# Four graph-attention layers on one core: a planner that knows transfer-behind-transfer and GpSimd-behind-VectorE waits, and a last feed-forward in column pieces

## The chip, the cores and the metric

The kernel runs on one core of a Trainium2 chip. The metric is the time of one execution on the device in microseconds; several executions give a median.

## The reference

The input x has 16 batches of 1024 nodes with 256 features, and adj is one 1024x1024 graph. Each of four layers adds a graph network of the normalized input to x:

```python
h = jnp.maximum(_layernorm(x, axis=-1), 0.0)
x = x + layer(h, adj, ...)
```

Layers 0 to 2 are graph attention (layer 0 with 4 heads of 64, layers 1 and 2 with one head of 256): project h, form scores from a source and a destination term with a leaky slope, mask with adj, softmax over the neighbours, weighted sum of the projected rows, then elu (layers 0, 2) or relu (layer 1). Layer 3 is a transformer block with 8 heads of 32:

```python
scores = jnp.where(mask, jnp.einsum('fnhd,fmhd->fhnm', q, k) / jnp.sqrt(D), -1e9)
t = jnp.einsum('fhnm,fmhd->fnhd', softmax(scores), v).reshape(F, N, C)
x = _layernorm(x + t, ln1_g, ln1_b)
h = jax.nn.relu(x @ w1 + b1)
x = _layernorm(x + h @ w2 + b2, ln2_g, ln2_b)
```

## The kernel before, in words

All work is recorded first and issued later. Each piece of work is a `Work` with an engine, an estimated time, the buffers it writes and reads, and a stream with a position. `Record.add` finds what each piece must follow. `Record.schedule` then plays the program through: it repeatedly takes the engine that can start something earliest, and on it the piece with the lowest key (the batch number plus a curve from `KNOTS` over the position in its stream, less a `LEAD`). What it plays is the order in which each engine's instructions are issued. [...] . `PASS` holds what the planner allows for handing a result from one engine to another. `SLACK` is added to each transfer, and `SWITCH` and `BIAS` price a change of the tile shape on TensorE.

Queues: SP issues all loads and stores. GpSimd issues the accumulating transfers of L1287 and runs small additions and the power -0.5 (L468, L483), which turns variances into inverse deviations.

Batches overlap: while one batch is in attention (layer 3) and its feed-forward, later batches are in layers 0 to 2. The names used below:

- Layers 0 to 2: `hn` is the normalized input, turned by TensorE (L531) and copied by ScalarE to `hT` (L788); L794 projects it; L805 and L816 evict into `e` and `qb`; L893 forms masked weights `pt` from a row `row` broadcast by SP (L876); L1007 and L1017 (layer 0, 128x32 tiles) and L920 (layers 1 and 2, full tiles) multiply; L940 to L977 finish and add to `xh`.
- Attention: L1157 projects keys and queries, L1166 and L1169 split them into `hi` and `lo`, SP stores them to `hl` (L1175) and loads them back in another arrangement as `qs` and `ks` (L1181). L1386 forms scores in four banks `sc`, L1410 takes exponentials into `pa`, L1419 masks them, L1243 multiplies with values and ones in 128x32 tiles, L1270, L1278 and L1287 add up pairs for the denominators. L1326, L531, L1346, L1353 and L1366 turn back, divide and add.
- Feed-forward (`feed`): L480, L483 and L492 give the inverse deviation, L502 normalizes, L531 turns, L1470 makes `yT`; L1483 multiplies with w1, L1504 evicts with relu into `fz`, L1483 multiplies with w2, L1521 adds to `yT` on VectorE. Then `back` turns `yT` (L531), evicts with sums (L1567, L448), and L1586 and L1599 combine with `xr`.
- `xr` is the residual of two node tiles: SP loads it from `x3` in HBM (L1536), VectorE adds the bias row (L1542), L1599 adds the result, SP stores it to the output (L1608). There are two `xr` buffers, so the load of a pair must wait for the store of the pair before the last.

The rule that decides which dependencies cost a hand-over in the plan is, for a writer behind earlier readers:

```python
for y in readers:
    if y is not x:
        x.before.setdefault(y, y.engine != engine)
```

In the plan all SP transfers belong to one engine, "dma".

Of the kernel before, what the change touches and what calls it, by code (L numbers as in the profile page):

```python
# [115 lines left out]
WEIGHT = {"pe": 1.0, "dve": 0.3}  # L116
PASS = {"pe": 0.198, "act": 0.161, "dve": 0.218, "pool": 0.13, "dma": 0.0}

# [25 lines left out]
class Record:  # L144
# [12 lines left out]
    def add(self, engine, us, emit, w=(), r=(), modes=("full", "full"), key=None, moved=0.0, lands=0.0):  # L157
# [4 lines left out]
        for wrote, refs in ((False, r), (True, w)):  # L162
            for ref in refs:
# [7 lines left out]
                for q in list(buf.parts) if part is None else {part, None}:  # L171
                    if q not in buf.parts:
                        continue
                    writer, readers = buf.parts[q]
                    if writer is not None and writer is not x:
                        x.before[writer] = x.before.get(writer, False) or (writer.engine, engine) != ("pe", "pe")
                    if wrote:
                        for y in readers:
                            if y is not x:
                                x.before.setdefault(y, y.engine != engine)  # L180
                if wrote:
# [7 lines left out]
    def schedule(self):  # L189
# [49 lines left out]

        order = []  # L240
        while True:
# [14 lines left out]
            if e == "pe":  # L256
                us += SWITCH.get((mode, x.modes[0]), 0.0)
                mode = x.modes[1]
            x.start = at
            if x.moved:  # L260
# [21 lines left out]
BEHIND, HELD = 2.0, 1.35  # L282
SLACK = 0.944
KNOTS = {
    "gat0": (-8.057, -7.567, -4.564, -6.528, -1.817, -1.899, -1.452, -3.246, -8.552),
    "gat1": (-2.024, -0.004, 0.215, 0.731, 0.959, 0.704, 0.611, 0.917, 0.899),
    "gat2": (1.118, -0.917, 0.633, 0.85, 0.97, 0.804, 1.307, 1.739, 1.201),
    "beside": (-0.565, 3.144, 4.806, -3.201, 8.62),
    "values": (-3.421, -4.341, -3.452, -4.286, -2.082, -2.123, 4.475, -0.299, 0.523),
    "steps": (-0.249, 0.878, 1.095, 1.509, 1.61, 1.967, 1.973, 2.318, 0.345),  # L290
    "feed": (4.232, 4.502, 1.869, 1.3, 2.54, 0.571, -2.425, 2.126, 2.697),
    "last": (4.663, 0.548, 4.755, 0.436, 4.627, 5.109, 4.463, 6.627, 6.529),
}
BIAS = 4.008
LEAD = {"act": 4.014, "dve": -5.116}

# [13 lines left out]
def tt_us(n):  # L310
    return (n / 0.96 + 67) / 1000


def stt_us(n):
    return (n / 0.96 + 128) / 1000

# [12 lines left out]
def direct(ctx, tc, flag, x, adj, gat_w, gat_a, w_qkv, ln1_g, ln1_b, ln2_g, ln2_b, w1, b1, w2, b2, out):  # L329
# [125 lines left out]
    def inverse_of_squares(mean, squares, rstd, refs, rstd_ref, negate=True):  # L455
# [10 lines left out]
        pool(  # L466
            1.6,
            lambda: nc.gpsimd.tensor_tensor(  # L468
# [8 lines left out]
    def inverse(mean, var, rstd, mv_refs, rstd_ref, negate=True):  # L477
# [3 lines left out]
        pool(  # L481
            1.6,
            lambda: nc.gpsimd.tensor_tensor(  # L483
# [23 lines left out]
    def watch(b_rec, view, k):  # L507
# [3 lines left out]
        pool(  # L511
            0.524,
            lambda: nc.gpsimd.tensor_tensor(
# [235 lines left out]
    def gat(xt, b_mv, b_rstd, l, my, squared):  # L749
# [8 lines left out]
        for hf in range(2):  # L758
# [76 lines left out]
            if H == 1:  # L835
# [6 lines left out]
            pool(  # L842
                1.0,
                lambda: nc.gpsimd.tensor_tensor(
# [63 lines left out]
        for hf in range(2):  # L908
# [83 lines left out]
            for h in range(0, H, 2):  # L992
# [64 lines left out]
                def sums():  # L1057
# [10 lines left out]
                dve(  # L1068
                    tt_us(HALF),
                    lambda: nc.vector.tensor_mul(  # L1070
# [36 lines left out]
    def attention(b, xt, b_mv, b_rstd):  # L1107
# [42 lines left out]
        def project(g, hf, keys, stack, at):  # L1150
# [4 lines left out]
            def product():  # L1155
# [11 lines left out]
            dve(  # L1167
                tt_us(HALF),
                lambda: nc.vector.tensor_sub(lo.t, sc.t, hi.t),  # L1169
# [88 lines left out]
        for n in range(len(steps) + LAG):  # L1258
# [62 lines left out]
            if m >= 0 and steps[m][2] == NT - 1:  # L1321
# [17 lines left out]
                def turned(u):  # L1339
# [11 lines left out]
                dve(  # L1351
                    tt_us(HALF),
                    lambda: nc.vector.tensor_mul(  # L1353
# [78 lines left out]
    def feed(b, x3, hn):  # L1432
# [4 lines left out]
        def turn(hf):  # L1437
# [18 lines left out]
            for ct in range(CT):  # L1456
# [22 lines left out]
                )  # L1479

        def product(g, co, w_sb, src):
            for ct in range(CT):
                nc.tensor.matmul(  # L1483
                    g.t,
                    w_sb[:, ct, co * P : (co + 1) * P],
                    src(ct),
                    start=ct == 0,
                    stop=ct == CT - 1,
                )

        def forward(hf):
            yT = yTs[hf]
            fT = [r_fz.new() for _ in range(CT)]
            for co in range(CT):
                g = r_bank.new()
                pe(
                    CT * mm_us(HALF),
                    lambda: product(g, co, w1_sb, lambda ct: yT.t[:, ct, :]),
                    [g, fT[co]],
                    [yT],  # L1500
                )
                act(
                    act_us(HALF, 1),
                    lambda: nc.scalar.activation(  # L1504
                        fT[co].t, g.t, AF.Relu, bias=cols["b1"][:, co : co + 1]
                    ),
                    [fT[co]],
                    [g],
                )
            for co in range(CT):  # L1510
                g = r_bank.new()
                pe(
                    CT * mm_us(HALF),
                    lambda: product(g, co, w2_sb, lambda ct: fT[ct].t),
                    [g],
                    fT,
                )
                u = yT.t[:, co, :]
                dve(
                    stt_us(HALF),  # L1520
                    lambda: nc.vector.scalar_tensor_tensor(  # L1521
                        u, g.t, cols["b2"][:, co : co + 1], u, op0=ALU.add, op1=ALU.add
                    ),
                    [yT(co)],
                    [g],
                )

        def back(hf):
            yT = yTs[hf]
            for it in (hf * TH, hf * TH + 2):  # L1530
# [31 lines left out]

                pe(0.109 * 2 * CT, turn_back, [g], [yT])
                for k in range(2):
# [744 lines left out]
```

## Time and profile before

| | us |
|---|---|
| median of three runs | 4072.89 (4071.52 to 4074.02) |
| profiled execution, its own time | 4064.23 |
| its span | 4062.4 |
| TensorE busy | 3971.5 |
| VectorE busy | 3617.2 |
| ScalarE busy | 2666.1 |
| GpSimd busy | 718.9 |

The profile is of one execution, 8.66 us below the median. Matmuls are pipelined and their ends are modelled, so a matmul that is held up counts as busy. Rows of the timeline give start, duration, engine, line, operation, operands, and in brackets the idle time of that engine just before, with what ended it. "SPq" is the issue of a transfer by SP.

### The profile page before, as it was taken

To read this page: it belongs to the slowest core of one execution; us is meant where nothing else is said; L and a number is where in the kernel's file an instruction comes from. 1 tells how busy PE (TensorE), PEld (TensorE's weight loads), DVE (VectorE), ACT (ScalarE), POOL (GpSimd) and SP (SyncE) were. 2 spreads that over 40 slices of the span, in tenths; PEclk is the share of its full clock that TensorE was granted. 3 is DMA by queue.
4 is the path that set the end of the run, shared out by engine and by line. 5 is a ranking of instruction groups with operands and counts; after the bars stand their busy time and mean duration, and the time that the engine had idled before them with its cause. 6 is when DMAs were issued, how large, how long until landed. Compare 5 with 4: busy or idle time off the path is not lost. (4 is left out here: it accounts for less than half of the span.)

```text
span 4062.4 us, 64901 instructions
## 1 busy us (share of the span) xinstructions
PE 3971.5 (98%) x23394; PEld 2330.7 (57%) x23394; DVE 3617.2 (89%) x6130; ACT 2666.1 (66%) x6639; POOL 718.9 (18%) x631
## 2 busy tenths in 40 slices
PE   7999999999999999999999999999999999999998
PEld 3556466564665646556565665646656465564653
DVE  7769998999989899898999999899998998989976
ACT  5356576675766757567665776757667575675675
POOL 1001121211212212121111212112122121211110
PEclk9999999999999999999999999999999999999999
DMA  3054454444544445354454544445444453544542
GB/s 128 24 148 115 120 135 110 103 106 117 136 112 104 107 120 133 104 124 107 111 121 121 133 115 100 106 117 133 115 104 104 118 137 104 122 103 103 124 130 60
DMA packets 228666, 460.65 MB, mean 113 GB/s; under 512 B 24816, under 2 KB 59888, under 8 KB 228336
## 3 DMA queue, kind: packets, MB, share of 16 engines
q1 hardware_dynamic: 193776, 330.58, 29.0%
q0 software_dynamic: 34560, 125.84, 16.0%
q8 instruction: 186, 3.05, 0.3%
q14 instruction: 144, 1.18, 0.1%
HBM read 229.45 MB, written 101.06 MB: 81 GB/s over the span
## 5 line engine op out<-in xcount | busy, mean ns | idle before, releaser
L1419 DVE TENSOR_TENSOR pa<-pa,mask 128x1024 f32<-128x1024 f32 x1024 | 1228.0, 1217 | 85.1 <-ACT pa L1410 83.4
L1410 ACT ACTIVATE pa<-sc 128x512 f32<-128x512 f32 x2048 | 1102.1, 602 | 296.7 <-PE sc L1386 206.5
L893 DVE SCALAR_TENSOR_TENSOR pt<-row,e,mask 128x512 f32<-128x512 f32 x1472 | 1008.0, 745 | 54.4 <-DMA row<-rd 38.9
L920 PE MATMUL bank<-qb,pt 128*128 128x257 f32 x4096 | 947.7, 381 | 1.6 <-DVE pt L893 1.4
L920 PEld LDWEIGHTS bank<-qb,pt 128*128 128x128 f32 x4096 | 772.5, 190 | 164.0 <-issue 23.3
L1386 PE MATMUL sc<-qs,ks 128*128 128x512 f32 x2048 | 742.3, 463 | 7.3 <-ACT pa L1410 5.5
L1243 PE MATMUL bank<-pa,va 128*32 128x512 f32 x4096 | 517.1, 598 | 0.1
L1386 PEld LDWEIGHTS sc<-qs,ks 128*128 128x128 f32 x2048 | 363.9, 189 | 196.3 <-ACT pa L1410 77.2
L1007 PE MATMUL bank<-pt,qb 128*32 128x512 f32 x3840 | 468.5, 598 | 2.7 <-DVE pt L893 1.5
L794 PE MATMUL bank<-w_aug,hT 128*128 128x259 f32 (+1 forms) x1504 | 388.6, 395 | 15.3 <-ACT hT L788 7.4
L1287 POOL DMA_DIRECT2D sums<-pa x240 | 213.9, 893 | 902.7 <-DVE pa L1419 269.5
L794 PEld LDWEIGHTS bank<-w_aug,hT 128*128 128x128 f32 x1504 | 273.6, 190 | 161.5 <-ACT pa L1410 26.0
L948 ACT ACTIVATE ex<-bank,rec 128x256 f32<-128x256 f32 x256 | 118.5, 474 | 344.0 <-DVE rec L940 343.8
L1270 DVE TENSOR_TENSOR sums<-pa,pa 128x1024 f32<-128x1024 f32 x240 | 289.1, 1220 | 26.5 <-PE bank L1243 26.5
L1278 DVE TENSOR_TENSOR sums<-sums,pa 128x1024 f32<-128x1024 f32 x240 | 290.9, 1218 | 21.1 <-DMA sums<-pa 21.0
L468 POOL TENSOR_TENSOR rstd<-rstd,neg_half 128x4 f32<-128x4 f32 x94 | 159.2, 1694 | 747.6 <-DVE rstd L460 747.6
L1007 PEld LDWEIGHTS bank<-pt,qb 128*32 128x32 f32 x3840 | 118.6, 110 | 283.9 <-issue 225.0
L1017 PE MATMUL bank<-pt,e 128*32 128x512 f32 x1920 | 257.6, 594 | 0.0
L1243 PEld LDWEIGHTS bank<-pa,va 128*32 128x32 f32 x4096 | 113.9, 109 | 249.1 <-issue 224.8
L1157 PE MATMUL sc<-hTa,wqkv_sb 128*128 128x512 f32 x512 | 243.4, 598 | 0.0
L1038 ACT COPY ot<-bank 128x512 f32<-128x512 f32 x120 | 70.3, 587 | 200.0 <-PE bank L1007 168.3
L502 ACT ACTIVATE hn<-xh,mv,rstd 128x256 f32<-128x256 f32 x376 | 197.8, 604 | 5.7 <-DVE mv L492 4.1
(153 smaller groups left out, 4695.3 us busy)
## 6 DMA issues: line engine op xcount, KB each, us to landing
sums<-pa POOLq DMA_DIRECT2D x240, 512.0 KB, 5.6
ks<-hl SPq DMA_DIRECT2D x256, 256.0 KB
qs<-hl SPq DMA_DIRECT2D x256, 256.0 KB
row<-rd SPq DMA_DIRECT2D x184, 256.0 KB
hl<-hi SPq DMA_DIRECT2D x128, 256.0 KB
hl<-lo SPq DMA_DIRECT2D x128, 256.0 KB
xh<-in_x_dram SPq DMA_DIRECT2D x32, 512.0 KB
x<-xh SPq DMA_DIRECT2D x32, 512.0 KB
```

Source lines behind the costliest of these rows:

```text
L794: nc.tensor.matmul(g.t[:, : C + 3 * H], hT.t[:, ct, k * P : (k + 1) * P], w_aug[l][:, ct, :], start=ct == 0, stop=ct == CT - 1,)
L893: lambda: nc.vector.scalar_tensor_tensor(pt.t, row.t, e3[:, 2, jt // TH, h, jt % TH : jt % TH + 1], mask[:, jt, hf * HALF : (hf + 1) * HAL ...
L920: nc.tensor.matmul(g.t[:, : D + 1], pts[jt].t[:, k * P : (k + 1) * P], qb[:, jt, 0, :], start=jt == 0, stop=jt == NT - 1,)
L1007: nc.tensor.matmul(g.t[u * D + d : u * D + d + D3, :], qb[:, j, h + u, d : d + D3], pts[u][j - jt].t, start=j == 0, stop=j == NT - 1,)
L1017: nc.tensor.matmul(gd.t[c : c + D3, :], one(jt + k, h + u).to_broadcast([P, D3]), pts[u][k].t, start=jt == 0, stop=jt == NT - 2,)
L1157: nc.tensor.matmul(sc.t, wqkv_sb[:, ct, c0 : c0 + P], hT.t[:, ct, hf * HALF : (hf + 1) * HALF], start=ct == 0, stop=ct == CT - 1,)
L1243: nc.tensor.matmul(ac.t[r * D3 : (r + 1) * D3, :], columns(r), of_head(r), start=first, stop=last,)
L1270: lambda: nc.vector.tensor_add(ss.t, p0.t, p1.t),
L1278: lambda: nc.vector.tensor_add(ss.t, ss.t, pt.t),
L1386: nc.tensor.matmul(scs[r - r0].t, ks.t[:, r, jt * P : (jt + 1) * P].bitcast(F32R), q.t[:, r, :].bitcast(F32R), start=True, stop=True,)
L1410: lambda: nc.scalar.activation(pt.t[:, v, :], sc.t, AF.Exp, scale=1.0 / math.sqrt(D3)),
L1419: lambda: nc.vector.tensor_mul(pt.t, pt.t, mask[:, jt : jt + 1, i0 : i0 + HALF].to_broadcast([P, 2, HALF]),),
```

## The change

It has three parts.

1. The planner. A writer that follows a transfer which reads its buffer is now planned to wait for that transfer's completion, even where the writer is itself a transfer. VectorE work with two operands in SBUF, and GpSimd additions and powers, carry a time of type `Port`. Where a GpSimd `Port` piece starts while a VectorE `Port` piece runs, the plan holds GpSimd until that VectorE instruction ends, or longer if another one follows at once. VectorE work that reads PSUM is marked `float`.
2. The constants: `PASS`, `SLACK`, `KNOTS`, `BIAS`, `LEAD` and the times of GpSimd's operations have other values. So the order on every engine is another one. Outside the last batch the same instructions are issued, transfers included.
3. In the last batch (b = 15) the products of the feed-forward are computed for 256 columns at a time: two pieces for each half of the nodes. Products, evictions (L1504) and additions (L1521) are made once for each piece, and the transposes behind them need only the piece that holds their columns.

```diff
-PASS = {"pe": 0.198, "act": 0.161, "dve": 0.218, "pool": 0.13, "dma": 0.0}
+PASS = {"pe": 0.156, "act": 0.266, "dve": 0.175, "pool": 0.13, "dma": 0.0}
+
+class Port(float):
+    pass
...
-                                x.before.setdefault(y, y.engine != engine)
+                                x.before.setdefault(y, y.engine != engine or y.moved > 0)
...
+        def hold(us):
+            free["pool"] += us
+            for y in held.after:
+                t = free["pool"] + held.pass_on
+                if held in y.before and y.before[held] and t > y.ready:
...
+                    y.ready = t
...
+            if e == "pool":
+                held = None
+                if isinstance(us, Port) and locked and free["dve"] > at:
+                    held, since, edge, long = x, at, free["dve"], last > 1.0
+                    us += edge - at - 0.05
+            if e == "dve":
+                locked = isinstance(us, Port)
+                if held:
+                    if locked and at <= edge + 0.02 and (edge - since < 0.35 or long and us > 1.0):
+                        hold(us)
+                        edge, long = at + us, us > 1.0
+                    else:
+                        held = None
+                last = us
...
-SLACK = 0.944
+SLACK = 0.748
...
-BIAS = 4.008
-LEAD = {"act": 4.014, "dve": -5.116}
+BIAS = 3.411
+LEAD = {"act": 1.749, "dve": -1.422}
...
 def tt_us(n):
-    return (n / 0.96 + 67) / 1000
+    return Port((n / 0.96 + 67) / 1000)
...
         pool(
-            1.6,
+            Port(0.4 + 0.15 * n),
...
+        PARTS = 2 if b == NB - 1 else 1
+        W = HALF // PARTS
...
+            for q in range(PARTS):
+                w = slice(q * W, (q + 1) * W)
+                for co in range(CT):
+                    g = r_bank.new()
+                    pe(
+                        CT * mm_us(W),
+                        lambda: product(g, co, w1_sb, lambda ct: yT.t[:, ct, w]),
+                        [g, fT[co](q)],
+                        [yT],
+                    )
...
+            for q in range(PARTS):
+                w = slice(q * W, (q + 1) * W)
+                for co in range(CT):
+                    g = r_bank.new()
+                    pe(
+                        CT * mm_us(W),
+                        lambda: product(g, co, w2_sb, lambda ct: fT[ct].t[:, w]),
+                        [g],
+                        [f(q) for f in fT],
+                    )
...
-                pe(0.109 * 2 * CT, turn_back, [g], [yT])
+                q = it % TH // 2 if PARTS == 2 else 0
+                pe(0.109 * 2 * CT, turn_back, [g], [yT((co, q)) for co in range(CT)])
```

The values of each curve in `KNOTS` differ as well.

## The prediction

> **What bounds the kernel now.** I read the busy times first, then one repeating stretch, then the waits of that stretch, then its timeline.
>
> ```profile
> PE 3971.5 (98%) x23394; PEld 2330.7 (57%) x23394; DVE 3617.2 (89%) x6130; ACT 2666.1 (66%) x6639; POOL 718.9 (18%) x631
> ```
>
> TensorE bounds the kernel. Its 98% does not mean that only 91 us (4062.4 - 3971.5) can be won, because a matmul that is held up still counts as busy. The order repeats exactly from batch to batch in the middle of the run. In the timeline the same late transpose returns at 570.1, 1310.9, 1558.4, 1805.1, 2051.9 us, so one batch takes 247 us.
>
> ```profile
> 1552.00:1799.00 247.00, 244.45 (x1449) 144.68 (x1448) 226.25 (x381) 166.30 (x417) 48.97 (x40) 1.00 0.47 116
> ```
>
> (Columns: stretch, length, busy PE, PEld, DVE, ACT, POOL.) The clock is full, and VectorE has 21 us free in 247. A microsecond saved in this stretch counts about fourteen times. Who stops TensorE and VectorE there, from 300 to 3900 us (total, times, longest):
>
> ```profile
> PE bank L531 <- DVE yT L1521: 16.9, 14, 1.7
> PE bank L794 <- ACT hT L788: 6.8, 15, 0.5
> PE bank L1483 <- ACT ex L948: 4.7, 9, 1.5
> PE bank L531 <- ACT pa L1410: 4.5, 14, 0.3
> ...
> DVE xr L1542 <- DMA xr<-x: 34.4, 14, 3.1
> ```
>
> The first and the last line are one story, once a batch:
>
> ```profile
> 1794.63 0.39 SPq L1608 DMA_DIRECT2D out_dram<-xr  x1
> 1798.92 0.32 SPq L1536 DMA_DIRECT2D xr<-x  x1
> ...
> 1802.93 0.69 DVE L1542 TENSOR_TENSOR xr<-xr,row_c 128x512 f32<-128x512 f32 x1 [2.74 <-DMA xr<-x]
> ...
> 1806.18 0.75 DVE L1521 SCALAR_TENSOR_TENSOR yT<-bank,col_b,yT 128x512 f32<-128x512 f32 x1
> ...
> 1806.98 0.98 PE L531 MATMUL bank<-ident,yT 128*128 128x128 f32 x7 [1.60 <-DVE yT L1521]
> ```
>
> The store of xr is issued at 1794.63. The load that refills xr must wait for the store to be complete and leaves at 1798.92 (4.29 later). Its data let VectorE go on at 1802.93 (4.01 later). Meanwhile VectorE stands 2.74 us at L1542 with both L1521 of the batch queued behind, and TensorE's transposes of yT stand 1.60 us.
>
> [...] the same 128x4 power on GpSimd takes from 1006 to 2650 ns, its shortest beside an idle VectorE. [...]
>
> **The change part by part.** No instruction changes except in the last batch; all else is order. Its steps, with the sum against the profiled time of 4064.23 us:
>
> 1. *A transfer's wait for another.* In the order before, both L1521 stand within five VectorE instructions behind an L1542 in 14 batches; in the order after, in none of the first thirteen batches: both L1521 precede the pair of L1542. The 16.9 us go. Ends: 0 and -20.7 (the whole run's total of that wait). What is late next: one new L1542 stands 7.7 us of VectorE work behind the last L1599 on its buffer. Counting VectorE's idle share that is about 8.4 us, against the 8.3 us from L1599's end (1794.61) to data (1802.93). The other follows 11.6 us of work. On SP the four qs loads now come between store and load, 4 x 0.44 us of issue, inside the 4.29 us that the load waits anyway. I charge nothing.
>
> 2. *Other hand-offs.* I summed TensorE's own work between a unit that feeds another engine and the unit that takes its result back, with each matmul at its start-to-start time in the trace. Per repeating batch six hand-offs had under 1.3 us of such cover (the tightest 0.46, hn to hT to L794); after, one (0.9, qb). In the batch from 1552 us the gaps in starts above the usual are 0.60 before L794, 0.46 before a transpose, 0.31 before L1483: 1.37 us, 19 us in 14 batches. I take 11 of them as gone. Ends: -19, and +10 if the new order makes new ones of that kind.
>
> 3. *Fewer changes of tile shape.* Runs of 32-column matmuls fall from 401 to 393. Entering one costs 0.094 us (203 against 109 ns after a transpose), leaving 0.206 (523 against 409, and 92 on the next weights): 8 x 0.30 = -2.4. Score runs (L1386) fall from 776 to 657, but one costs nothing beyond its matmuls: 28 + 421 + 234 ns from the last projection's start, against 216 + 2 x 232.
>
> 4. *First 300 us.* Scores stand bunched at 262 to 300 us and TensorE waits 6.0 us there for exponentials and a qs load. The new order puts L920 between most of them. I take -4; ends -12 and +6, since 13 more shape changes (145 against 132) lie there.
>
> 5. *Last batch's feed-forward.* Columns go in two pieces for each half: 16 matmuls more, the same total time on TensorE; ScalarE 8 x 0.478 - 4 x 0.685 = +1.1 us, VectorE 8 x 0.481 - 4 x 0.74 = +0.9 us (rows of 256 elements). Now the tail:
>
> ```profile
> 4048.69 0.69 DVE L1542 TENSOR_TENSOR xr<-xr,row_c 128x512 f32<-128x512 f32 x1 [2.66 <-DMA xr<-x]
> 4049.30 0.74 DVE L1521 SCALAR_TENSOR_TENSOR yT<-bank,col_b,yT 128x512 f32<-128x512 f32 x1
> ...
> 4050.10 1.76 PE L531 MATMUL bank<-ident,yT 128*128 128x128 f32 x7 [3.03 <-DVE yT L1521]
> ```
>
> Three of four pieces of the last yT now precede L1542, and the transposes of the first piece need no later one. Against that, the other half's four pieces (1.9 us) stand on VectorE among the statistics that lead to L480 and xh, which makes the last half start about 1.9 us later. It then meets fewer stops. Following both chains I get -2.2; ends -5 and +2.
>
> 6. *Costs of the new order.* VectorE has 171 more separate semaphore waits (1099 against 928), 21 ns each in the row of L1542: 3.6 us of its 445 us idle. The cover is thin in the 95% slices, so I charge +3 (ends 0 and +8). GpSimd's new entry in the planner costs nothing: TensorE waits 12.7 us for GpSimd once, at the start, and that stays.
>
> Sum: -16.9 - 11 - 2.4 - 4 - 2.2 + 3 = -33.5 us, 4030.7 in the profile. The median shown is 8.66 above the profiled run, so 4072.89 - 33.5 = 4039 us.
>
> **The rivals.** About 0.2% (8 us) is what a measurement of this kernel can tell from no change.
>
> *Slower: VectorE's stop only moves.* If the four qs loads must wait on SP for their own store (SP waits 197.6 us in 74 times for hl, 2.7 each), the xr load leaves later and VectorE stands at the new L1542, with two masks (L1419) and the reciprocal that frees the accumulators behind. Before, a stop of 2.74 cost TensorE 1.6 to 1.8, so 0.62 per us. The gain is 2.4 us a batch; a stop over 3.9 us eats it. At 5.4 us: 14 x 3.3 - 33.5 = +13, 4086 us. [...] Against: hl's stores are issued just ahead of the xr store and should be done when it is. 13%.
>
> *The waits are exchanged.* Step 1 holds, but as many new hand-offs are late as went: -16.9 + 10 + 5 = about -2, 4071 us. For it: VectorE at 91% of the batch always has something late. Against: the six tight hand-offs are one. 7%.
>
> *All of it goes.* The ends of steps 1 to 5 without new costs: -20.7 - 19 - 2.4 - 12 - 5 = -59, 4014 us. 13%.
>
> *The change does not act* on GpSimd: the order would still be this one. It is part of the likeliest case.
>
> **How the numbers follow.** The likeliest case (67%) gives 4039 us, on its own 4022 to 4058. Faster by over 0.2% are this case and "all of it": 0.80. Within 0.2%: 0.07. Slower: 0.13. The range that leaves out two in ten takes half of "all of it" and the exchange: 4016 to 4071.
>
> **What would show it.** Right: the wait of L531 for L1521 is under 4 us from 300 to 3900; L1542 stops VectorE under 10 us in total; a batch repeats in 244.5 to 245.5 us; scores and their waits before 300 us shrink. Wrong: L1542 among VectorE's longest waits still, TensorE's wait for L1386's scores or L794 grown, or a period at 247 us or more.

## The result, and the profile after

| | before | after |
|---|---|---|
| median, us | 4073.45 (4 runs, 4071.52 to 4079.68) | 4022.16 (4 runs, 4019.40 to 4024.49) |
| ratio, 95% interval | | 0.9871 [0.9854, 0.9888] |
| profiled execution, its own time, us | 4064.23 | 4019.40 |
| its span, us | 4062.4 | 4017.6 |

The change makes the kernel 51.3 us faster by the medians, and 44.8 us by the two profiled spans. The forecast was 4039 us, with a range from 4016 to 4071. The sign was right and the time lies in the range, but the gain came out larger than its sum of 33.5 us, and only in part by the sum's own steps. The profiled execution of before, 4064.23 us, is faster than every other execution of that kernel in this document, so what is read from its trace understates the gain.

Line numbers of the changed kernel are some 30 to 40 higher: L531 is L562, L1521 is L1562, L1542 is L1583, L1386 is L1417, L1410 is L1441, L860 is L891, L893 is L924, L468 and L475 are L499 and L506. The experiments' numbers lie between 0 and 3 off those of the kernel that they start from.

The busy times of the page after:

```profile
PE 3953.2 (98%) x23426; PEld 2331.5 (58%) x23426; DVE 3620.1 (90%) x6134; ACT 2660.7 (66%) x6643; POOL 664.7 (17%) x631
```

TensorE's share is still 98%. Its busy time fell by 18.3 us with 32 matmul instructions more (the program's 16 matmuls, two instructions each). So part of what is booked as busy was waiting, as the prediction said of this number, or ran at half clock (below). The waits of TensorE from 300 to 3900 us (total, times, longest), after:

```profile
PE bank L891 <- DVE yT L1562: 10.9, 13, 0.8
PE bank L1274 <- ACT rt L897: 5.0, 12, 0.4
PE sc L1417 <- ACT pa L1441: 2.2, 5, 0.8
PE bank L951 <- ACT qb L847: 1.9, 8, 0.2
```

And VectorE's for the reloaded residual:

```profile
DVE xr L1583 <- DMA xr<-x: 0.5, 1, 0.5
```

The four lines of before are gone: L531 for L1521 (16.9), L794 for `hT` (6.8), L1483 for `ex` (4.7) and L531 for `pa` (4.5). VectorE's 34.4 us at the bias row are 0.5. But the first line is new: another TensorE instruction now waits for the same addition, once a batch. It is read below. Of the prediction's signs, the four of being right came (a batch repeats in 245.1 us); of those of being wrong one did in a small way, the scores' wait for exponentials, 0.7 us before (L1386) and 2.2 after (L1417).

To see where the time was won, I take the start of the first, the 256th, the 1792nd and the last score matmul (L1386, L1417; 128 for each batch) from the traces. Between the 256th and the 1792nd lie twelve batches.

| us | first score | 256th | 1792nd | last | span | the twelve batches | last score to end |
|---|---|---|---|---|---|---|---|
| before | 263.5 | 681.4 | 3644.3 | 4020.4 | 4062.4 | 2962.9 | 42.0 |
| after | 251.9 | 659.4 | 3600.5 | 3978.0 | 4017.6 | 2941.1 | 39.6 |
| b_swap | 263.8 | 676.6 | 3623.8 | 3999.6 | 4041.7 | 2947.2 | 42.1 |
| b_moved | 263.6 | 677.6 | 3619.3 | 3994.1 | 4034.7 | 2941.7 | 40.6 |
| b_swap_rec | 264.9 | 678.7 | 3626.1 | 4005.1 | 4046.9 | 2947.4 | 41.8 |
| b_warm | 258.7 | 676.8 | 3651.6 | 4032.7 | 4074.3 | 2974.7 | 41.6 |
| b_moved_warm | 255.9 | 668.2 | 3609.9 | 3984.2 | 4024.7 | 2941.7 | 40.5 |
| a_ref | 252.9 | 661.8 | 3602.7 | 3980.1 | 4021.7 | 2940.9 | 41.6 |
| a_parts1 | 256.3 | 665.3 | 3606.2 | 3983.7 | 4026.3 | 2940.9 | 42.6 |
| a_early | 253.1 | 659.2 | 3590.2 | 3967.6 | 4008.7 | 2931.0 | 41.1 |
| a_nohold | 262.1 | 684.8 | 3701.2 | 4101.6 | 4138.1 | 3016.4 | 36.5 |
| b_consts | 259.0 | 695.4 | 3798.8 | 4205.5 | 4244.4 | 3103.4 | 38.9 |

So 22.0 of the 44.8 us are won up to the 256th score, 21.8 in the twelve repeating batches (246.9 to 245.1 us each) and 1.0 behind them. In these two profiles the start has as large a share as the whole steady part, and that is where the forecast was far off. In a slower execution of before's steady order (b_warm) the twelve batches take 2974.7 us, 33.6 more than after, so in such an execution the steady part's share is the larger one.

The start, in windows (stretch, length, busy PE, PEld, DVE, ACT, POOL; then the granted TensorE clock, the share of DMA, GB/s). Before, then after:

```profile
50.00:100.00 50.00, 43.96 (x315) 18.03 (x319) 42.12 (x86) 24.27 (x73) 6.30 (x6) 0.90 0.31 93
100.00:150.00 50.00, 43.85 (x309) 22.33 (x302) 39.42 (x89) 13.95 (x36) 3.27 (x4) 0.93 0.10 32
250.00:300.00 50.00, 43.26 (x175) 22.47 (x173) 33.00 (x35) 26.09 (x58) 3.87 (x5) 0.93 0.69 166
```

```profile
50.00:100.00 50.00, 46.15 (x378) 18.86 (x370) 45.05 (x87) 22.65 (x68) 4.42 (x6) 1.00 0.24 70
100.00:150.00 50.00, 44.49 (x278) 26.24 (x270) 39.72 (x95) 14.68 (x37) 6.93 (x4) 0.93 0.12 32
250.00:300.00 50.00, 49.57 (x248) 29.42 (x247) 47.59 (x59) 30.22 (x58) 4.54 (x5) 1.00 0.64 150
```

Two things change. TensorE is busy longer from 250 to 300 us, where the scores stood bunched. And the clock, which the prediction called full from a window in the steady part, is not full in the start before: the trace has it at one half for 3.4 us from 70.0, and for 6.8 us each from 90.5, 121.2 and 285.0, together 23.8 us. After, it has 6.8 us, from 112.2. 17 us less of half clock are worth up to 8.5 us. TensorE's stops of over 0.1 us sum to 42.1 us up to the 256th score before, and to 30.7 after. These 11.4 us and the 8.5 make 19.9 of the start's 22.0. Beside the waits around the scores (6.0 us up to 300 us before, 0.4 after) those for L1063 (L1094 after) shrank most; from 0 to 100 us they are in the kernel before

```profile
PE bank L860 <- DVE rec L1063: 3.2, 1, 3.2
PE bank L531 <- DVE rec L1063: 2.7, 1, 2.7
```

and 0.7 us after.

### The profile page after: what moved, and what is told of

It is laid out like the page before. It is cut to its first block, busy times and chain, and to the rows that moved or that the text cites. A ratio compares the mean times of both kernels' runs of the same rounds, so it can differ in the third digit from the quotient of the medians.

```text
span 4017.6 us, 65083 instructions
## 1 busy us (share of the span) xinstructions
PE 3953.2 (98%) x23426; PEld 2331.5 (58%) x23426; DVE 3620.1 (90%) x6134; ACT 2660.7 (66%) x6643; POOL 664.7 (17%) x631
## 4 chain that ended last, share of the span: by engine, by line
PE 84%; ACT 7%; DVE 5%; issue 2%; DMA 2%; SPq 0%; DVEq 0%; ACTq 0%; POOLq 0%
PE bank L951 20%; PE bank L1274 11%; PE bank L1038 11%; PE sc L1417 10%; PE bank L825 6%; PE bank L1517 5%; PE bank L562 5%; PE bank L1048 5%; PE sc L1188 5%; PE sc L1226 3%; ACT pa L1441 3%; ACT hn L533 1%; DMA sums<-pa 1%; DVE sums L1301 1%; ACT waste L479 1%
## 5 line engine op out<-in xcount | busy, mean ns | idle before, releaser
L1450 DVE TENSOR_TENSOR pa<-pa,mask 128x1024 f32<-128x1024 f32 x1024 | 1227.7, 1220 | 52.8 <-ACT pa L1441 50.0
L1441 ACT ACTIVATE pa<-sc 128x512 f32<-128x512 f32 x2048 | 1099.8, 606 | 197.5 <-PE sc L1417 130.9
L924 DVE SCALAR_TENSOR_TENSOR pt<-row,e,mask 128x512 f32<-128x512 f32 x1472 | 1012.4, 747 | 58.0 <-DMA row<-rd 32.8
L1417 PE MATMUL sc<-qs,ks 128*128 128x512 f32 x2048 | 699.3, 449 | 2.7 <-ACT pa L1441 2.6
L1274 PE MATMUL bank<-pa,va 128*32 128x512 f32 x4096 | 515.5, 598 | 0.0
L1417 PEld LDWEIGHTS sc<-qs,ks 128*128 128x128 f32 x2048 | 362.6, 189 | 173.9 <-issue 54.1
L1038 PE MATMUL bank<-pt,qb 128*32 128x512 f32 x3840 | 459.4, 594 | 0.7 <-DVE rec L1094 0.4
L825 PE MATMUL bank<-w_aug,hT 128*128 128x259 f32 (+1 forms) x1504 | 380.3, 394 | 7.4 <-DVE w_aug L649 3.2
L825 PEld LDWEIGHTS bank<-w_aug,hT 128*128 128x128 f32 x1504 | 274.5, 190 | 136.0 <-ACT qb L847 27.6
L1274 PEld LDWEIGHTS bank<-pa,va 128*32 128x32 f32 x4096 | 110.4, 109 | 241.8 <-issue 209.6
L499 POOL TENSOR_TENSOR rstd<-rstd,neg_half 128x4 f32<-128x4 f32 x94 | 161.7, 1720 | 385.7 <-DVE rstd L491 288.0
L1197 ACT CAST hi<-sc 128x512 fp32r<-128x512 f32 x128 | 74.7, 583 | 204.8 <-PE sc L1188 188.0
```

The source lines that it names most:

```text
L825: nc.tensor.matmul(g.t[:, : C + 3 * H], hT.t[:, ct, k * P : (k + 1) * P], w_aug[l][:, ct, :], start=ct == 0, stop=ct == CT - 1,)
L924: lambda: nc.vector.scalar_tensor_tensor(pt.t, row.t, e3[:, 2, jt // TH, h, jt % TH : jt % TH + 1], mask[:, jt, hf * HALF : (hf + 1) * HAL ...
L1038: nc.tensor.matmul(g.t[u * D + d : u * D + d + D3, :], qb[:, j, h + u, d : d + D3], pts[u][j - jt].t, start=j == 0, stop=j == NT - 1,)
L1274: nc.tensor.matmul(ac.t[r * D3 : (r + 1) * D3, :], columns(r), of_head(r), start=first, stop=last,)
L1417: nc.tensor.matmul(scs[r - r0].t, ks.t[:, r, jt * P : (jt + 1) * P].bitcast(F32R), q.t[:, r, :].bitcast(F32R), start=True, stop=True,)
L1441: lambda: nc.scalar.activation(pt.t[:, v, :], sc.t, AF.Exp, scale=1.0 / math.sqrt(D3)),
```

## The experiments

The theory after the result had three parts. A: the planner's knowledge that a transfer waits for a transfer carries the steady gain, by the stop at the bias row. B: the start's gain is TensorE's stops and the half clock that follows them. C: the rest of the change's other hand-offs were exchanged for new ones. Rivals: the constants alone carry it; GpSimd's entry in the planner is idle, as the prediction had it; the pieces of the last feed-forward carry a share.

### b_swap: 14 bias rows behind the additions, order of before otherwise

```diff
+for x in [w for w in order if w.tag == "bias"]:
+    line = [w for w in order if w.engine == "dve"]
+    n = line.index(x)
+    adds = [w for w in line[n + 1 : n + 6] if w.tag and w.tag[0] == "add"]
+    if len(adds) == 2:
+        moved(x, order.index(x), order.index(adds[1]))
```

> The kernel before with one thing moved: in 14 batches the addition of the bias row (L1542) that stood ahead of both additions to yT (L1521) on VectorE now stands behind the second; every other order is that of before. Theory A (the wait of a transfer for another one reached TensorE through this place): TensorE's wait for L1521, 16.9 us from 300 to 3900, goes, VectorE's stop of 34.4 us at the bias row shrinks to under 10, and the time falls by 14 to 20 us, to about 4056. Rival (such waits are only exchanged): VectorE stops as long a few instructions later and another TensorE wait grows, and the time falls by under 6 us, 4067 to 4073.

Measured: 4046.82 us (4043.45 to 4048.41), ratio to the kernel before 0.9918 [0.9904, 0.9931]; span 4041.7, 20.7 us under that of before. VectorE's wait for the reload and TensorE's for L1521 are gone from both lists. L1483's wait for `ex` stays (4.1 us after 4.7). The twelve batches gain 15.7 us. This shows the mechanism of step 1 alone, at the size of its lower end in the spans; by the medians it brings 33.3 us (4080.08 beside it), for a reason that the base for the median below gives.

### b_moved: one token of the planner

```diff
-x.before.setdefault(y, y.engine != engine)
+x.before.setdefault(y, y.engine != engine or y.moved > 0)
```

> The kernel before with one token of the change: a writer behind a transfer that reads its buffer is planned to wait for it (or y.moved > 0); all constants as before. In its order no addition to yT stands close behind a bias row, and runs of 32-column matmuls stay 401. Theory A (the knowledge of that wait alone brings what the reordering by hand brought): the profiled span within 5 us of 4041.7, the wait of TensorE for yT's last addition gone, median 4040 to 4050. Rival B (the planner pays for it elsewhere, since constants were tuned without it): span at 4052 or more, with new waits of TensorE above 10 us in total between 300 and 3900 us.

Measured: 4036.61 us (4034.38 to 4038.49), 0.9896 [0.9883, 0.9908]; span 4034.7. That is 27.7 us of the 44.8 by span. By the medians of one series it is 41.4 of 55.0 (4077.96 before, 4022.99 for the changed kernel, a_ref). It fits theory A except that the median, 4036.61, and the span, 7.0 below 4041.7, lie past its better ends. TensorE's waits from 300 to 3900 us:

```profile
PE bank L794 <- ACT hT L788: 6.7, 15, 0.5
PE bank L531 <- ACT pa L1410: 4.5, 14, 0.3
PE bank L1007 <- DVE rec L1063: 1.2, 3, 0.5
PE bank L1483 <- ACT ex L948: 0.8, 5, 0.2
```

L1483's 4.7 us have fallen to 0.8 as well. In the twelve batches 14.4 us of L531's wait and 3.1 of L1483's are gone, 17.5 of the 21.2 us that they gained; the other 3.7 are not in these lists. With the constants and everything else of before, the twelve batches take 2941.7 us. The whole change takes 2941.1. So **the token alone brings the steady gain**; what the rest of the change adds there comes to nothing in the sum.

### a_early: the addition ahead of L506 in the changed kernel

In the changed kernel's new wait the chain can be read in the timeline:

```profile
1506.85 2.61 POOL L499 TENSOR_TENSOR rstd<-rstd,neg_half 128x4 f32<-128x4 f32 x1 [7.67 <-DVE rstd L491]
...
1507.34 1.23 DVE L1450 TENSOR_TENSOR pa<-pa,mask 128x1024 f32<-128x1024 f32 x1
...
1509.49 0.16 DVE L506 TENSOR_TENSOR mv<-mv,rstd 128x4 f32<-128x4 f32 x1 [0.93 <-POOL rstd L499]
...
1509.57 1.22 DVE L1450 TENSOR_TENSOR pa<-pa,mask 128x1024 f32<-128x1024 f32 x1
...
1510.71 0.74 DVE L1562 SCALAR_TENSOR_TENSOR yT<-bank,col_b,yT 128x512 f32<-128x512 f32 x1
...
1511.51 0.27 PE L891 MATMUL bank<-ident,e 128*4 128x128 f32 x1 [0.84 <-DVE yT L1562]
```

GpSimd's power took 2.61 us; its end, 1509.46, lies 0.9 behind the end of the mask L1450 (1507.34 + 1.23). VectorE stood 0.93 us at L506 for it. The addition L1562, two places behind, came late by that, and TensorE stood 0.84 us for the bank that the addition frees. The experiment puts the addition first ("neg" marks L506):

```diff
+for x in [w for w in order if w.tag == ("add", 1, 1)]:
+    line = [w for w in order if w.engine == "dve"]
+    n = line.index(x)
+    negs = [w for w in line[n - 3 : n] if w.tag == "neg"]
...
+        moved(x, order.index(x), order.index(negs[0]))
```

> The changed kernel with one thing moved: the last addition to yT (L1562 there) of each repeating batch, which stood behind the product of mean and inverse deviation (L506) and a mask, now stands ahead of them. In the changed kernel VectorE stands 0.93 us at L506 for GpSimd's power (which took 2.61 us beside a mask instruction), and TensorE then waits 0.84 us a batch for the bank that this addition reads. Theory A (that chain is a wait that remained): TensorE's wait of 10.9 us in 13 goes and the time falls by 9 to 13 us against the changed kernel, 4009 to 4013. Rival (L506 being 0.75 us later delays the normalized rows instead): within 4 us of the changed kernel, 4018 to 4026.

Measured: 4010.47 us (4009.98 to 4016.21), 0.9830 [0.9816, 0.9845]; span 4008.7, 8.9 under that of the changed kernel. The twelve batches take 2931.0 instead of 2941.1: the 10.9 us of this wait are won nearly in full. TensorE's longest totals from 300 to 3900 us are now

```profile
PE bank L1276 <- ACT rt L899: 5.0, 12, 0.4
PE sc L1419 <- ACT pa L1443: 3.5, 6, 1.1
PE bank L953 <- ACT qb L849: 2.3, 10, 0.2
```

So the changed kernel had given about 10 us back to one new stop. With it gone, the twelve batches take 10.7 us less than b_moved's, though TensorE's listed waits are about as long (10.1 us against 11.0). So the rest of the change does win in the steady part, and this stop hid it. There are 276 runs of 32-column matmuls in these batches against 288 in b_moved, 3.6 us at the price of step 3; where the rest lies is open.

### a_nohold: the planner never holds GpSimd

```diff
-if isinstance(us, Port) and locked and free["dve"] > at:
+if False:
```

> The changed kernel whose planner never holds GpSimd for VectorE's running instruction (the times of GpSimd stay as changed). Its order has 431 runs of 32-column matmuls against 393. Theory A (the hold matters only through the order that it leads to): 38 x 0.30 = 11 us slower than the changed kernel, 4028 to 4040. Rival B (it costs nothing and brings nothing): within 4 us of 4022. Rival C (real stops behind GpSimd appear as well): above 4040, with VectorE's waits for rstd at L506 and L523 grown by over 10 us.

Measured: 4137.81 us (4134.12 to 4139.97), 1.0151 [1.0137, 1.0165]. Rival C, far beyond theory A's 11 us: 115 us slower than a_ref, the changed kernel in another series. Each of the twelve batches takes 251.4 us. VectorE's waits for GpSimd from 300 to 3900 us:

```profile
DVE mv L523 <- POOL rstd L514: 47.6, 42, 1.2
DVE mv L506 <- POOL rstd L499: 35.6, 55, 0.9
```

In the changed kernel these two are

```profile
DVE mv L506 <- POOL rstd L499: 12.1, 13, 0.9
DVE mv L523 <- POOL rstd L514: 9.7, 16, 1.6
```

and TensorE's longest total in a_nohold is for ScalarE's exponentials:

```profile
PE sc L1188 <- ACT pa L1441: 24.5, 15, 1.8
PE sc L1417 <- ACT pa L1441: 12.9, 16, 3.3
```

GpSimd's entry is not idle. With the short times that the change gives to the powers (1.0 for four columns, where before had 1.6) the plan needs the hold; without it VectorE comes to results before they are ready. How that reaches the exponentials, and through them TensorE, was not followed. One number in it misleads: L514's power takes 1138 ns on average here and 1741 in the changed kernel. It is shorter where VectorE stands and waits for it: in the changed kernel the 20 of these powers that VectorE waited for took 1.06 us on average and the other 46 took 2.04, and here VectorE waits for 42 of them where it waited for 16. The bill isn't closed: the listed waits of TensorE in 300 to 3900 us are 60 us against 22 (+38), 38 more shape runs at 0.30 make 11, and 20.5 us of half clock between 1595 and 3965 us, where the changed kernel has none, make up to 10. That is 59 of 115, and the twelve batches alone lost 75. The run also doesn't tell what the old flat 1.6 without hold would have cost in the changed planner; b_consts has both, but not the token.

### b_consts: the new constants in the old planner

The planner's rules, GpSimd's times and the whole feed-forward are those of before; `KNOTS` are those of the change too.

```diff
-PASS = {"pe": 0.198, "act": 0.161, "dve": 0.218, "pool": 0.13, "dma": 0.0}
+PASS = {"pe": 0.156, "act": 0.266, "dve": 0.175, "pool": 0.13, "dma": 0.0}
...
-SLACK = 0.944
+SLACK = 0.748
...
-BIAS = 4.008
-LEAD = {"act": 4.014, "dve": -5.116}
+BIAS = 3.411
+LEAD = {"act": 1.749, "dve": -1.422}
```

> The changed constants in the planner of before: PASS, SLACK, KNOTS, BIAS, LEAD as changed, but neither the wait of a transfer for a transfer nor the hold of GpSimd, and GpSimd's times as before; feed-forward whole. Its order has 458 runs of 32-column matmuls against 393, and in about half of the batches a bias row stands again close ahead of additions to yT. Theory A (constants alone bring the start, knowledge the rest): first score within 4 us of 252, but the whole 4045 to 4080. Rival B (the constants carry the gain): below 4035. Rival C (the start too needs the knowledge): first score after 259.

Measured: 4245.24 us (4243.26 to 4246.21), 1.0415 [1.0399, 1.0431]. None of the three expected so much. The first score comes at 259.0, so the constants bring 4.5 us up to there, not 11.6, and at the 256th score nothing is left: it comes 14.0 us later than before. The twelve batches take 258.6 us each. TensorE waits for exponentials (32.8 us in 38 times at L1386), and for masks (9.1), `qb` (8.6) and masked weights (7.2) besides. **The constants alone carry none of the gain.** They were set for another planner, which is the likely reason. How the loss of 170 us divides over the missing pieces of knowledge was not tried, nor the new rules with the old constants beyond the token.

### b_warm, b_moved_warm and a_warm: filler work in the early stops

Filler transposes (128x128, into a score bank not yet in use) are issued just ahead of the instruction that TensorE waits with. They fill the stop, and the order of everything else stays. `FILL` has the number of the matmul and how many fillers go ahead of it. b_warm's, shown here, are 96 (the expectation says 92); b_moved_warm has 92, 22 at 307.

```diff
+FILL = {226: 22, 307: 26, 420: 22, 421: 26}
...
+                    if seen[0] in FILL:
+                        n = FILL.pop(seen[0])
...
+                        for _ in range(n):
+                            tr(r_sc.tiles[0][:, :P], ident, ident)
```

> The kernel before with 92 transposes of the identity into an unused bank put ahead of the four TensorE units that wait longest in the first 125 us (22, 26, 22 and 26 of them, 2.4 to 2.8 us each, inside waits of 2.7 to 3.3 us); nothing else differs and nothing reads them. Theory B (a TensorE stop of some 3 us is followed by a window at half clock, 3.4 to 6.8 us long, and this is a part of the 22 us that the changed kernel gains before the second batch ends): the windows at half clock at 70, 90.5 and 121 us go, and the time falls by up to half their 17 us, 6 to 9 us, to about 4065. Rival (the clock is low for another reason, or the work after such a stop isn't bound by TensorE): the windows stay or the time stays within 3 us of before.

Measured: 4073.52 us (4064.32 to 4082.14), 0.9980 [0.9972, 0.9989], so 6.6 us under the 4080.08 of the kernel before beside it by the medians, 8 by the ratio. The windows of the start (same columns):

```profile
50.00:100.00 50.00, 48.25 (x394) 24.23 (x398) 44.96 (x91) 25.67 (x76) 6.23 (x6) 1.00 0.34 103
100.00:150.00 50.00, 49.10 (x355) 29.39 (x348) 40.92 (x94) 13.92 (x36) 3.06 (x4) 1.00 0.11 32
```

The clock is full where it was 0.90 and 0.93. Up to the first score 3.4 us of half clock are left (at 36.5 us) of 17.1, worth up to 6.8; that score comes 4.8 us earlier. The interval is wide for 8 us because before's own order scatters (see below), so the same was done to b_moved, whose runs lie closer.

> b_moved (median 4036.6, span 4034.7, first score at 263.6 us) with 92 filler transposes in TensorE's four longest early stops, at about 70, 92, 118 and 122 us; they write a score bank that is not in use yet. Theory A (half of the start's gain was stretches of half clock that follow stops): the stretches at 69.7 and 117.5 us (13.6 us together) are gone, the first score comes 4 to 7 us earlier, and the median falls by 4 to 8 us. Rival B (the clock is no part of it, or the stretches come back at shorter stops): first score within 2 us of 263.6.

Measured: 4032.05 us (4026.53 to 4034.42), 0.9896 [0.9881, 0.9911], against 4036.61 (4034.38 to 4038.49) of b_moved in another series; span 4024.7, 10.0 less. The half clock before 320 us fell from 27.2 to 3.4 us, which at half rate is worth up to 11.9. The first score starts at 255.9 instead of 263.6, 7.7 us earlier, a little more than theory A's 4 to 7. But stretches at 21.9, 260.9 and 295.0 us, 13.6 us of the 27.2, have no filler near them. And the ratios to the kernel before beside each are the same, 0.9896, so the 4.6 us between the medians aren't clear of the two series. The first score agrees with a clock part; b_warm, with its kernel before in the same series, is what shows it.

> The changed kernel with 42 such transposes ahead of its two longest waits (2.0 and 3.25 us, at 109 to 115 us); nothing reads them. Theory B: its window at half clock at 112 us (6.8 us) goes and the time falls by about 3 us, to 4019. Rival: window or time stay, 4022.

Here 42 fillers stand at the changed kernel's two stops behind `w_aug` (16 and 26). Measured: 4020.07 us (4017.54 to 4022.61), 0.9849 [0.9835, 0.9862], 2 us under the changed kernel in another series: inconclusive. The stretch at 112 us went, but its profile has 3.4 us of half clock at 86.8, 247.2 and 308.7 instead.

### b_swap_rec: two early sums ahead of masks

It starts from b_swap. `x` are the sums, and the numbers are places in VectorE's order.

```diff
+for x, ahead in ((line[102], line[99]), (line[142], line[138])):
+    moved(x, order.index(x), order.index(ahead))
```

> The kernel before with the 14 bias rows moved behind the additions (as in the earlier run, span 4041.7, median 4046.8), and two more VectorE instructions moved: the sums L1063 that TensorE waited for at 69.1 us (2.74) and 91.4 us (3.16) go ahead of three and four instructions, mostly masks L893. Theory A (the start's gain is stops of TensorE and the half-clock stretches that follow stops of about 3 us): both stops fall under 1.2 us, the stretches of half clock at 70 and 90.5 us are gone (they cost 1.7 and 3.4 us), and the first score comes 6 to 10 us earlier than 263.5 us. Rival B (VectorE is full there, so TensorE waits as long for the masks that were passed): first score less than 3 us earlier, the stops moved to L1007 or L1017 behind L893.

Measured: 4047.94 us (4045.92 to 4050.27), 0.9923 [0.9911, 0.9935]; first score at 264.9, 1.1 us later than in b_swap. TensorE's waits from 50 to 130 us:

```profile
PE bank L1007 <- DVE va L825: 2.7, 1, 2.7
PE bank L531 <- DVE rec L1067: 1.6, 1, 1.6
PE bank L531 <- DVE rec L1063: 0.8, 1, 0.8
PE bank L860 <- DVE rec L1063: 0.6, 1, 0.6
```

The waits for the sums fell from 2.7 and 3.2 to 0.8 and 0.6, and TensorE stood 2.7 and 1.6 us for L825 and L1067, which still stand behind the masks. A stretch of half clock of 6.8 us begins at 89.3 us, where b_swap had none. The run's rival B is right: these two moves don't take the early stops away, they hand them on. Which part of the new order shortens them in the changed kernel was not shown.

### a_ref and a_parts1: the last feed-forward whole again

```diff
-PARTS = 2 if b == NB - 1 else 1
+PARTS = 1
```

> The changed kernel itself, as the base for its variants on this chip. Both theories: 4018 to 4026 us, ratio to the kernel before 0.984 to 0.989.

> The changed kernel with the last batch's feed-forward in whole halves again (PARTS = 1), everything else as changed. Theory A (the pieces are worth what the prediction's fifth step said, about 2 us, and the tail from the last score became 1.0 us shorter in the two profiles): 1 to 4 us slower than the changed kernel. Rival B (the 16 extra matmuls and extra evictions cost as much as the earlier start brings, and the 1.0 us came from the order): within 1 us of it or faster.

Measured in one series: a_ref 4022.99 us (4021.51 to 4023.69), 0.9861 [0.9847, 0.9876]; a_parts1 4026.16 (4023.16 to 4028.02), 0.9868 [0.9853, 0.9882]. The medians differ by 3.2 us, as theory A wanted, but the traces put it elsewhere. TensorE's order of the two is the same up to the last batch's feed-forward. Yet the first score comes 3.4 us later in a_parts1, whose trace has 13.6 us of half clock before 320 us against 6.8; half of 6.8 is the 3.4. From the last score to the end it is 42.6 against 41.6 us, and 39.6 in the first profile of the same kernel. Of these last 2.0 us half clock accounts for up to 1.7: at 3996.7 us a stretch lasts 6.8 us in a_ref and 3.4 in the first profile (in a_parts1 none stands there). So the pieces are worth about 1 to 3 us, and these runs can't separate that from how the tail varies.

### a_best: a_early with fillers

It is a_early with these fillers.

```diff
+FILL = {146: 10, 230: 8, 308: 8, 420: 16, 421: 26, 14064: 14}
```

> The changed kernel with the last addition to yT ahead of L506 (median 4010.5 in the earlier run) and 82 filler transposes in six of its stops (five before 117 us, one at 3984 us). Theory A: the stretches of half clock at 113 (6.8 us) and 3984 us (6.8) go, 2 to 6 us faster, 4004 to 4009. Rival B (such stretches appear at other, shorter stops instead, as in the earlier fill of the changed kernel): 4009 to 4013.

Measured: 4009.76 us (4006.87 to 4012.47), 0.9837 [0.9824, 0.9851]. The half clock before the final stretch fell from 13.6 us (a_early) to 3.4, but the time only by 0.7 us against another series: rival B's range. What beats both kernels is a_early's one move; the fillers on top add nothing that these runs show.

## Why the prediction was right, and where its steps failed

Its main mechanism, step 1, is shown. That the time fell into the range, at the edge of its likeliest case (4022 to 4058), is in part luck: by the profiles step 4 brought 18 us more than it was priced at, and of step 2's 11 us nothing is left in the steady part.

**Step 1, the transfer's wait for another (-16.9).** Right in its place and its mechanism, and too small. The two waits that it named fell to nothing, b_swap showed them by themselves (-20.7 in span), and b_moved showed the token with -27.7. L1483's 4.7 us of waits for `ex`, which the prediction booked as another hand-off, stayed when only the stop was removed (4.1 in b_swap) and went with the token's order (0.8 in b_moved). The new L1542 behind L1599 was charged nothing, rightly: 0.5 us. The rival that the stop only moves is refuted by the same line.

**Base for the median (+8.66).** The sum was made in the profile and carried to the median as if the 8.66 us between them stayed. Most of it was part of what was taken away. The kernel before scattered from 4066.80 to 4091.84 in the 27 runs beside the first experiments, b_swap from 4043.45 to 4048.41. b_warm's profiled execution (4076.21 us) has the same steady order as before, and there the stop was larger (waits of TensorE, whose line is that of a wrapper, then of VectorE):

```profile
PE bank L1712 <- DVE yT L1521: 24.2, 19, 1.7
```

```profile
DVE xr L1542 <- DMA xr<-x: 42.4, 14, 4.0
```

against 16.9 and 34.4 in the profile of before. Beside it the clock fell as well, at 1558.8 (6.8 us), 3047.0 and 3791.2 (3.4 each), where the profile of before has none:

```profile
1559.46 1.75 PE L1712 MATMUL bank<-ident,yT 128*128 128x128 f32 x7 [1.66 <-DVE yT L1521]
```

```profile
1550.00:1570.00 20.00, 17.14 (x76) 9.10 (x75) 13.75 (x27) 8.09 (x29) 0.86 (x1) 0.83 0.32 79
```

(The columns of the second line are those of the start's windows; 0.83 is the clock.) Within its twelve batches the stop is 6.3 us longer in total (20.7 against 14.4), and 10.2 us at half clock are worth up to 5.1: 11.4 of the 11.8 us by which these batches are longer. The 27 runs fit this: 18 with a mean clock of 0.994 take 4082.3 us on average, seven with 0.995 take 4077.1. So the profiled execution was a lucky one in the very term that the change removes, and the prediction's 1.60 us for each stop left out what the stop can cost by the clock.

**Step 2, other hand-offs (-11).** The old ones went as predicted: 11.3 us of L794 for `hT` and L531 for `pa`, beside the 4.7 of L1483. What failed is "after, one": the count looked at TensorE's own work between a unit and its return, and couldn't see a bank that VectorE frees late because VectorE itself waits for GpSimd. With 10.9 us at L891, 5.0 at L1274 and 6.7 in smaller waits, nothing is left of it in the steady part: b_moved still has those 11.2 us, in the twelve batches it waits 8.0 us less than the changed kernel (11.0 against 19.0), and takes the same 2941 us. The rival of exchanged waits was right for this step and wrong for step 1.

**Step 3, tile shapes (-2.4).** Not separated by an experiment. In the twelve batches 12 runs fewer go with part of a_early's 10.7 us over b_moved, which has before's 401.

**Step 4, the first 300 us (-4).** This is the mis-sized term: -22.0 up to the 256th score in the first pair of profiles, -19.6 in a_ref, of which the token brings 3.8 (b_moved). Its own range ended at -12. The prediction saw 6.0 us of waits around the scores and stopped there. It read the clock of one steady window and not that of the start, where the three windows shown above stood at 0.90 to 0.93; 17 us less of it are worth up to 8.5, and filling the stops of before gave 6.6 by the medians (b_warm). It also looked at the scores alone, and passed over 5.9 us of waits for L1063 before 100 us, which are 0.7 after. The 13 more shape changes, its upper end, didn't show: the traces count 158 before and 157 after, up to the 256th score.

**Step 5, the last batch's pieces (-2.2).** Compatible: from the last score to the end, the two profiles of the changed kernel are 0.4 and 2.4 us shorter than before and 1.0 and 3.0 shorter than a_parts1. The runs don't prove more.

**Step 6, costs (+3).** The 21 ns for each wait were not separated. "GpSimd's new entry in the planner costs nothing" rested on TensorE's own waits for GpSimd, of which there is one, at the start. That was the wrong place to look: without the hold these constants take 115 us longer, and with it a GpSimd power still costs the changed kernel the 10.9 us of L891, through VectorE's queue. The power's 2.61 us beside a mask (after, at 1506.85) stand against 1.01 us of the same power where VectorE is idle (before, at 61.8 us). Of the 94 powers of L468 in the trace before, the 17 with no VectorE instruction beside them took 1.01 to 1.02 us, the other 77 took 1.01 to 2.65, 1.84 on average. The prediction's "its shortest beside an idle VectorE" is not exact: another of 1.01 us, at 53.5, ran beside an L893, which has two inputs in SBUF. So not every overlap lengthens it, and which does was not tested.

## What to carry to other kernels

Telling a planner of one real wait can win more than new weights: here one token gave 27.7 us of span, while the new constants without the new rules lost 170. When a stop is removed, follow the waiting engine's whole queue, over the engine that serves it, to what is late next, and read the granted clock in each stage, above all in the start, before calling it full. And price a forecast's base as well: if the removed wait is the one that varies, the profiled run isn't typical of it.

## What the runs showed of the hardware

In these traces a stop of TensorE can cost more than its length: in b_warm's twelve batches the stops at L1521's addition are 6.3 us longer in total than before's, and 10.2 us at half clock, which the profile of before doesn't have there, are worth up to 5.1 us more. Ahead of the stretch that runs to the end, the stretches of half clock in the profiles before and after last 3.41 or 6.83 us. In the kernel before they start at 69.98, 90.46, 121.18 and 285.02 us: 20.48, 30.72 and 163.84 us apart, which is 6, 9 and 48 times 3.413 us, the length of the shortest. The stops that go with them can be shorter than that: in the kernel before, stops of 2.74 and 3.16 us stand at the first two of these stretches; in b_warm's steady part, stops of 1.2 and 1.66 us close together at one of 6.8.

What goes with half clock in these two profiles is the sum of the stops within such a step of 3.413 us. Both traces, cut into steps from a start of half clock, up to the last four, have five steps at full clock that hold over 2 us without a matmul (ends of matmuls as modelled): 2.53, 2.23, 2.77 and 2.91 us before, in the steps from 66.6, 87.0, 117.8 and 281.6 us, and 2.63 us after, in the step from 108.8. Half clock begins at the end of each. Of 52 steps with 0.5 to 1.67 us, one is followed by half clock (after, 1.67 us in the step from 3993.2); of 2279 with less, none. So one stop can fall into one step or be parted between two, as the stop of 3.16 us is (2.23 and 0.93), which fits that other stops are hit from run to run of one order. It can cost some us: a_parts1 and a_ref have the same order up to the last feed-forward, and the first scores lie 3.4 us apart, with 13.6 and 6.8 us of half clock before 320 us.
